# A macaron block on one core: written order for the routing stages' side engines, and an earlier logits' transpose in the attention

## The chip, the core and the metric

The kernel runs on one core of a Trainium2 chip. A core has five engines that run side by side, each with its own list of instructions: TensorE (PE in the profile) for matrix products, VectorE (DVE), ScalarE (ACT), GpSimd (POOL), and SyncE (SP), which here only starts transfers. The engines wait for one another by semaphores. The metric is the time of one execution on the device in microseconds (us), the median of several.

## The reference

The input X has 16 sequences of 256 tokens with 256 channels, in float32: 4096 tokens. The block is a half step of a feed-forward layer, an attention, and another half step of the same feed-forward layer:

```
x = x + 0.5 * ffn(layernorm(x))
x = x + attention(layernorm(x))
x = x + 0.5 * ffn(layernorm(x))
```

The feed-forward layer contains its own input in its output, so that a half step gives x + LN(x)/2 plus half of two sums. It first scales its input h to n = w_norm * h / rms(h). A router takes softmax(n @ w_router) over 32 experts and picks the best four for each token. Each expert takes at most 128 tokens (the first ones in token order; later ones are dropped) and computes silu(n @ w_gate) * (n @ w_up) @ w_down with a width of 176, weighted by the token's probability. A shared expert of width 704 runs over all tokens, weighted by sigmoid(n @ w_shared_gate).

The attention has 16 query heads and 8 key heads of 32 channels, rotary positions on q and k, scores scaled by 1/16 and bent by 50*tanh(s/50), a causal mask, a softmax, and an output projection Wo.

## The kernel before

**Tiles and stages.** The tokens lie in SBUF as 32 tiles x of 128 tokens (NT), in 8 groups of four (NG, GT). The kernel goes through five stages:

1. *First routing stage* (about 0 to 113 us). For each group, `route` (from line 237) computes layernorm statistics on DVE (`moments`, L226 and L227), inverse roots of them on POOL (`root`, L234), and the normed rows xr on DVE (L257). PE transposes xr into pt (L274), and ACT writes that scaled into xnT (L277), from which all matrix products of the layer start. PE makes the router's logits plt (L291); ACT copies them to lt (L296); DVE makes the shared expert's gate by four products with wg (junk, L300). PE transposes the logits to pl (L306), DVE takes the maximum (mx, L308) and subtracts it (ex, L310), ACT takes the exponential (L312), and DVE makes the probabilities and the choice of four (tot L315 to mask L334). `mixed` (L261) makes x + LN(x)/2 in place, by ACT, one instruction for each of the four tiles.
2. *First expert stage* (about 113 to 335 us). With the masks of all groups, PE counts positions (pc, L350), DVE and POOL make the lists of tokens, and each expert's tokens are gathered from a table in memory (xtab) by POOL's indirect DMA, computed (`expert`, pge L467, poe L480) and added back to a sum in memory by another indirect DMA (acc, L483). POOL runs these in written order.
3. *Attention* (about 335 to 800 us). Units (g, b, m) are half of the heads of one sequence. For unit k the loop at line 801 writes: the late sums of unit k−1 (plate, L604), the first part of the scores (sc, L582), the output projection of an earlier unit (poa, L646), projections of the next group (`project`: pq L533, then on DVE a shuffle qs L536, a multiply L540 and further adds), the rest of the scores, and the softmax sums and values of unit k−1 (den and y L628, dT L631, yT L636). Steps of the second layer's routing for groups that are done, `advance(routing.get(...))`, stand between these.
4. *Second expert stage* (from about 809 us), as the first.
5. *Tail*: the sums are read back from memory (a<-acc, L491) and added to x (L495 by POOL, L788 by DVE), and the rest of the shared expert (pg L420, tanh L424, act L425 and L426, po L432, the add into x L436) goes out with the result.

**The shared expert as filler.** The shared expert is a chain of steps without a deadline of their own. The class `Fill` (L657) hands them out in written order: each call of `take(us)` adds to a budget and issues steps until the budget is used up. A step of pg is booked at 3.4, one of po at 2.6. An expert step adds EXPERT_FILL.

**What sets the order.** PE runs in written order throughout (L101). DVE, ACT and POOL run in written order only inside the stack `ordered` (L757 to L882), which covers the attention. POOL also does so in the expert stages. Everywhere else a planner at build time orders DVE's, ACT's and POOL's instructions. Buffers limit this further. PSUM has a ring of two for pg and sc ("big"), one of two named "mm" (pt, po, pq, poa) and one of two named "aux". The logits' tiles plt and pl lie in "aux", but in the second layer's routing, except for its last group, in "mm" (`bank`, L242): the same ring as the projections' pq.

**Lines around the change.** wg, the product of the shared gate's weights with w_norm, is made at line 149 from a copy of w_norm that is loaded into x's last tile. triu, the triangle for the position counts, is made at line 161, and first read by pc. mixed() is called at line 333 in the first layer, and after the first half of the transposes (L283) in the second. Each `yield` in `route` ends one step of it; `feed_forward` (L696) and the attention's loop call the steps.

## Time and profile before

| | us |
|---|---|
| median of three runs | 1091.03 (1089.23 to 1092.94) |
| the profiled execution's own time | 1094.7 |
| its span, first to last instruction | 1093.0 |
| PE busy in it | 1029.6 |
| DVE busy | 647.4 |
| ACT busy | 402.8 |
| POOL busy | 497.1 |
| mean granted clock of PE | 0.981 of full speed |

"L306" in the profile is line 306 of the kernel before. A row like `PE pl L306 <- DVE kT L540` says that PE stood idle ahead of its instruction at line 306 until DVE's at line 540 had ended. A row of the timeline begins with start and length, then names engine, line, operation, and what is written from what; matmuls that follow without a gap are put together (x8), and the bracket is the idle time before the first of them, with what ended it. A window's row gives busy time of each engine in a stretch of time, and PEclk, the share of full clock that PE was granted there.

### The profile page before, as it was taken

How to read it: one execution, taken by the hardware profiler on the slowest of the kernel's cores; microseconds unless marked ns; L12 is line 12 of the kernel's file. 1: busy time of each engine (PE TensorE's matmuls, PEld its weight loads, DVE VectorE, ACT ScalarE, POOL GpSimd, SP SyncE). 2: the span in 40 equal slices, each digit the busy share in tenths (PEclk: the TensorE clock that was granted, in tenths of full speed). 3: DMA queues.
4: the chain of work that ended last, by engine and by line, in shares of the span. 5: the costliest groups of instructions: out<-in, count | busy, mean ns of one | idle time of the engine just before them, and what ended most of it. 6: DMA issues, size and time to landing. Idle time of an engine off the chain costs nothing.

```text
span 1093.0 us, 15757 instructions
## 1 busy us (share of the span) xinstructions
PE 1029.6 (94%) x5448; PEld 633.1 (58%) x5448; DVE 647.4 (59%) x1782; ACT 402.8 (37%) x777; POOL 497.1 (45%) x548
## 2 busy tenths in 40 slices
PE   7799999999999999998989898999899999999988
PEld 4456546776866545444545454555456576867655
DVE  4885664434443546777777868785757644444343
ACT  3343111222220256583738374758221122222101
POOL 3330101555553477786666666574101245555350
PEclk9999999999999999999999999999999999999989
DMA  9631701878862000000101010000300167877380
GB/s 272 201 121 50 238 1 47 174 166 173 176 146 44 19 20 18 3 20 2 41 1 43 1 42 1 23 22 1 97 28 1 33 144 162 179 167 174 49 287 20
DMA packets 137887, 93.13 MB, mean 85 GB/s; under 512 B 80272, under 2 KB 135120, under 8 KB 137808
## 3 DMA queue, kind: packets, MB, share of 16 engines
q1 hardware_dynamic: 125520, 74.29, 24.6%
q0 software_dynamic: 12288, 17.83, 9.5%
q8 instruction: 44, 0.72, 0.3%
q14 instruction: 35, 0.29, 0.1%
HBM read 61.12 MB, written 30.97 MB: 84 GB/s over the span
## 4 chain that ended last, share of the span: by engine, by line
PE 55%; DVE 9%; ACT 2%; DMA 2%; issue 1%; SPq 0%; POOL 0%; DVEq 0%; ACTq 0%; POOLq 0%
PE pg L420 14%; PE po L432 9%; PE pq L533 6%; PE poa L646 5%; PE sc L582 5%; PE pge L467 4%; PE y L628 3%; PE den L628 3%; PE poe L480 2%; DVE st L226 1%; DMA acc<-y,idx 1%; PE pv L561 1%; DVE junk L300 1%; DMA a<-acc 1%; DVE mv L227 1%
## 5 line engine op out<-in xcount | busy, mean ns | idle before, releaser
L420 PE MATMUL pg<-xnT,sw 128*128 128x512 f32 x704 | 320.0, 600 | 4.3 <-DVE act L426 4.3
L420 PEld LDWEIGHTS pg<-xnT,sw 128*128 128x128 f32 x704 | 131.0, 191 | 144.9 <-issue 135.6
L432 PE MATMUL po<-swd,act 128*128 128x256 f32 x768 | 185.3, 393 | 7.9 <-DVE x L436 2.8
L483 POOL DMA_INDIRECT acc<-y,idx x64 | 101.4, 1584 | 178.3 <-DVE y L482 93.6
L432 PEld LDWEIGHTS po<-swd,act 128*128 128x128 f32 x768 | 147.3, 196 | 38.3 <-issue 11.1
L424 ACT ACTIVATE act<-pg 128x512 f32<-128x512 f32 x96 | 57.2, 596 | 299.5 <-PE pg L420 281.5
L425 DVE SCALAR_TENSOR_TENSOR act<-act,pg 128x512 f32<-128x512 f32 x96 | 65.8, 685 | 143.3 <-ACT act L424 117.6
L589 ACT ACTIVATE p<-sc 128x512 f32<-128x512 f32 (+1 forms) x128 | 97.0, 808 | 107.0 <-PE sc L582 106.4
L467 PE MATMUL pge<-xgT,wgu 128*112 128x128 f32 (+1 forms) x768 | 96.1, 275 | 9.3 <-issue 4.8
L594 POOL TENSOR_SCALAR_AFFINE_SELECT p<-p 128x512 f32<-128x512 f32 x128 | 83.7, 677 | 45.1 <-ACT p L592 41.4
L592 ACT ACTIVATE p<-p 128x512 f32<-128x512 f32 (+1 forms) x128 | 100.9, 845 | 0.0
L443 POOL DMA_INDIRECT xg<-xtab,idx x64 | 68.1, 1064 | 71.8 <-DVE idx L397 52.9
L467 PEld LDWEIGHTS pge<-xgT,wgu 128*112 128x112 f32 (+1 forms) x768 | 88.7, 182 | 13.7 <-issue 10.8
L436 DVE SCALAR_TENSOR_TENSOR x<-po,sg,x 128x256 f32<-128x256 f32 x64 | 30.9, 483 | 75.9 <-PE po L432 66.2
L541 POOL TENSOR_TENSOR qs<-qs,kc 128x512 f32<-128x512 f32 x48 | 61.3, 1276 | 20.1 <-DVE qs L536 20.1
L462 ACT ACTIVATE xgT<-pte,wnorm 128x128 f32<-128x128 f32 x128 | 39.7, 365 | 76.6 <-PE pte L459 59.8
L582 PE MATMUL sc<-qT,kT 32*128 32x256 f32 (+1 forms) x512 | 66.3, 550 | 1.7 <-ACT p L589 1.3
L426 DVE TENSOR_TENSOR act<-act,pg 128x512 f32<-128x512 f32 x96 | 65.7, 685 | 2.3
L480 PE MATMUL poe<-wd,sie 112*128 112x256 f32 x256 | 66.0, 380 | 0.9 <-DVE sie L474 0.9
L646 PE MATMUL poa<-wo,yT 128*128 128x256 f32 x256 | 61.6, 394 | 4.4 <-DVE yT L636 3.1
L646 PEld LDWEIGHTS poa<-wo,yT 128*128 128x128 f32 x256 | 48.3, 194 | 22.8 <-DVE yT L636 5.1
L533 PE MATMUL pq<-hT,wq 128*128 128x512 f32 x128 | 60.9, 599 | 0.0
(113 smaller groups left out, 1339.0 us busy)
## 6 DMA issues: line engine op xcount, KB each, us to landing
xtab<-xr SPq DMA_DIRECT2D x16, 576.0 KB
acc<-zero SPq DMA_DIRECT2D x2, 4224.0 KB
a<-acc SPq DMA_DIRECT2D x16, 512.0 KB
wgu<-in_L_ffn_w_gate SPq DMA_DIRECT2D x64, 112.0 KB
wgu<-in_L_ffn_w_up SPq DMA_DIRECT2D x64, 112.0 KB
wd<-in_L_ffn_w_down SPq DMA_DIRECT2D x64, 112.0 KB
wgu<-in_L_ffn_w_gate SPq DMA_DIRECT2D x64, 64.0 KB
wgu<-in_L_ffn_w_up SPq DMA_DIRECT2D x64, 64.0 KB
```

The costliest lines, as they stand in the source:

```text
L420: nc.tensor.matmul(pg[:, s, :], lhsT=sw[:, c, w0 : w0 + P], rhs=xnT[:, c, cols], start=(c == 0), stop=(c == 1))
L432: nc.tensor.matmul(po, lhsT=act[:, k, t * P : (t + 1) * P], rhs=swd[:, k, :], start=(k == 0), stop=(k == len(FC) - 1),)
L443: nc.gpsimd.indirect_dma_start(out=xg, out_offset=None, in_=xtab[n], in_offset=bass.IndirectOffsetOnAxis(ap=idx[:, e : e + 1], axis=0), bo ...
L467: nc.tensor.matmul(pg[:fw, n_, :], lhsT=wgu[:, c, w0 : w0 + fw], rhs=xgT[:, c, :], start=(c == 0), stop=(c == 1))
L480: nc.tensor.matmul(po, lhsT=si[:, k, :], rhs=wd[:, k, :], start=(k == 0), stop=(k == 1))
L483: nc.gpsimd.indirect_dma_start(out=acc[n], out_offset=bass.IndirectOffsetOnAxis(ap=idx[:, e : e + 1], axis=0), in_=y, in_offset=None, boun ...
L533: nc.tensor.matmul(pq, lhsT=weights[:, c, :], rhs=hT[:, c, :], start=(c == 0), stop=(c == 1))
L582: nc.tensor.matmul(sc[i // 2][:, i % 2, 0 : 2 * w].rearrange("p (s t) -> p s t", s=2), lhsT=kT[r, m, t0 + k0 : t0 + k0 + P], rhs=qT[r, m, ...
L589: nc.scalar.activation(parts[h], sc[h][:, :, 0 : 2 * w], AF.Tanh, scale=QK_SCALE / SOFTCAP)
L592: nc.scalar.activation(parts[h], parts[h], AF.Exp, scale=SOFTCAP)
L594: nc.gpsimd.affine_select(out=diag, in_=diag, compare_op=ALU.is_ge, fill=0.0, base=0, pattern=[[0, 4], [1, P]], channel_multiplier=-1,)
L646: nc.tensor.matmul(po, lhsT=yT[:, c // 2, c % 2, qh * P : (qh + 1) * P], rhs=wo[:, c // 2, c % 2, :], start=(c == 0), stop=(c == 3),)
```

## The change

The diff has these edits. EXPERT_FILL goes from 2.15 to 2.3. A tile wn of its own takes w_norm, and the product for wg is written just ahead of the first group's junk. triu is made after the routing loop. In the first layer, mixed() leaves its place between the choice of four and the mask; it becomes a step of its own behind the mask, and is called one group later. In `feed_forward` the whole routing loop runs inside a manual schedule for DVE, ACT and POOL, so that these engines take its instructions in written order. In the attention's loop, the routing step that makes pl, mx and ex stands at j == 2 directly behind the first part of the scores, ahead of the output projection and the projections; at j == 3 the routing step of group g−2 (tot to mask) stays where it was before the last group, and in the last units (k > LAST) it comes ahead of the filler's step.

```diff
-ROUTE_FILL, SLOT_FILL, FIRST_FILL, EXPERT_FILL, SUM_FILL, PROJECT_FILL = 2.0, 1.7, 6.0, 2.15, 17.0, 1.5
+ROUTE_FILL, SLOT_FILL, FIRST_FILL, EXPERT_FILL, SUM_FILL, PROJECT_FILL = 2.0, 1.7, 6.0, 2.3, 17.0, 1.5
...
-    nc.sync.dma_start(x[:, NT - 1, :], w_norm.unsqueeze(0).to_broadcast([P, C]))
-    nc.vector.tensor_mul(wg, wg, x[:, NT - 1, :])
+    rows0 = ExitStack()
+    xrows = rows0.enter_context(tc.tile_pool(name="rows0", bufs=3, side="right"))
+    wn = xrows.tile([P, C], F32, name="wn", bufs=1)
+    nc.sync.dma_start(wn, w_norm.unsqueeze(0).to_broadcast([P, C]))
...
-    nc.vector.tensor_single_scalar(triu, const("iota"), slot, ALU.is_ge)
...
         nc.scalar.copy(lt, plt)
+        if n == 0 and g == 0:
+            nc.vector.tensor_mul(wg, wg, wn)
         for t in range(GT):
...
-        if n == 0:
-            mixed()
         nc.vector.tensor_single_scalar(
             mask[:, :, g * GT : (g + 1) * GT], hit[:, :, 0:E].rearrange("p t e -> p e t"), 1.5, ALU.is_gt
         )
         yield 0.0
+        if n == 0:
+            mixed()
+            yield 0.0
...
-        for g, work in works.items():
...
-            advance(work, 1 + n)
-            advance(later[1])
...
+        with tc.manual_schedule(engines={ET.DVE, ET.Activation, ET.Pool}):
+            for g, work in works.items():
...
+                advance(work, 1 + n)
+                advance(works.get(g - 1))
+                advance(later[1])
...
+            advance(work, 1 - n)
         if n == 0:
             routed.close()
+
+            nc.vector.tensor_single_scalar(triu, const("iota"), slot, ALU.is_ge)
             clear(0)
             load_attention()
...
                 next(parts)
+            if j == 2:
+                advance(routing.get(g - 2))
             if k >= 2 and units[k - 2][2] == 1:
                 d = units[k - 2][:2]
                 project_out(*d, outs.pop(d))
             advance(mine, PROJECT_PIECES[j][0])
             if k == LAST:
                 fill2.step()
-            if j == 2:
-                advance(routing.get(g - 2))
...
+            if j == 3 and k > LAST:
+                advance(routing.get(g - 2))
...
-            if j == 3:
+            if j == 3 and k < LAST:
                 advance(routing.get(g - 2))
```

More of the change, by code (lines that the diff above doesn't have):

```diff
@@ L696, in feed_forward @@
     def feed_forward(n, pool, works, fill, routed=None):
-        for g, work in works.items():
-            later = [works.get(g + d) for d in range(3)]
-            next(work)
-            if g == 0:
-                next(later[1])
-            fill.take(ROUTE_FILL)
-            advance(work, 1 + n)
-            advance(later[1])
-            if n == 0 and g == 0:
-                warm(WARM[1])
-            fill.take(ROUTE_FILL)
-            next(work)
-            fill.ready = g + 1
-            fill.take(LOGIT_FILL)
-            advance(work, 2)
-            advance(later[2])
-            fill.take(ROUTE_FILL)
-            next(work)
+        with tc.manual_schedule(engines={ET.DVE, ET.Activation, ET.Pool}):
+            for g, work in works.items():
+                later = [works.get(g + d) for d in range(3)]
+                next(work)
+                if g == 0:
+                    next(later[1])
+                fill.take(ROUTE_FILL)
+                advance(work, 1 + n)
+                advance(works.get(g - 1))
+                advance(later[1])
+                if n == 0 and g == 0:
+                    warm(WARM[1])
+                fill.take(ROUTE_FILL)
+                next(work)
+                fill.ready = g + 1
+                fill.take(LOGIT_FILL)
+                advance(work, 2)
+                advance(later[2])
+                fill.take(ROUTE_FILL)
+                next(work)
+            advance(work, 1 - n)
         if n == 0:
             routed.close()
+            nc.vector.tensor_single_scalar(triu, const("iota"), slot, ALU.is_ge)
             clear(0)
@@ L749, in macaron_kernel @@
     with tc.tile_pool(name="ffn0", bufs=1) as pool:
-        rows0 = ExitStack()
-        xrows = rows0.enter_context(tc.tile_pool(name="rows0", bufs=3, side="right"))
         first = {g: route(0, g, xrows) for g in range(NG)}
```

## The prediction

> **What bounds the kernel now.** I read the busy shares first, then what ended TensorE's idle time, then the lines around the longest of those waits, and last the granted clock in short windows.

> ```profile
> PE 1029.6 (94%) x5448; PEld 633.1 (58%) x5448; DVE 647.4 (59%) x1782; ACT 402.8 (37%) x777; POOL 497.1 (45%) x548
> ```

> TensorE (PE) is busy for 1029.6 of 1093.0 us; no other engine passes 60%. The diff takes no matmul away, so it can act only on PE's 63 us of idle time and on the stretches at half clock. The waits of PE (total, times, longest) name the idle places:

> ```profile
> PE pl L306 <- DVE kT L540: 14.5, 5, 3.3
> ...
> PE pg L420 <- DVE act L426: 4.3, 2, 3.5
> ...
> PE poa L646 <- DVE yT L636: 3.1, 1, 3.1
> PE po L432 <- DVE x L436: 2.8, 1, 2.8
> ...
> PE po L432 <- ACT xnT L277: 2.1, 1, 2.1
> PE pc L350 <- DVE mask L334: 1.6, 1, 1.6
> ```

> The diff touches each of them: the first in the attention, the third where the attention ends, the po behind x in the tail, the rest in the first routing stage.

> **1. Attention: pl (the logits' transpose) goes ahead of the projections.** Of the five places I show the one at 561, PE and then VectorE (DVE); columns are start, length, engine, line.

> ```profile
> 561.00 0.33 PE L306 MATMUL pl<-kc,lt 128*128 128x128 f32 x1 [3.32 <-DVE kT L540]
> 561.26 1.24 PE L582 MATMUL sc<-qT,kT 32*128 32x256 f32 x8
> 559.66 0.72 DVE L536 STREAM_SHUFFLE qs<-pq 128x512 f32<-128x512 f32 x1
> 560.27 0.67 DVE L540 TENSOR_TENSOR kT<-pq,kc 128x512 f32<-128x512 f32 x1
> 562.40 0.29 DVE L310 TENSOR_TENSOR ex<-pl,mx 128x128 f32<-128x128 f32 x1
> ```

> pl and the projections' tiles pq share a PSUM ring of two. Today the order on the ring is pq of k, pq of the first q, pl; pl must wait until kT's multiply (L540) has read the first of them. That multiply stands on DVE behind eight pairs of layernorm statistics and the late sums' add (plate, L604), whose end at 559.66 I call P. The scores' second part stands behind pl on PE and starts at P + 1.60.

> After the change the order is pl, pq of k, pq of q. pl finds a free bank and its own 3.32 us go. But now the q projection takes pl's bank, so it waits until pl's readers mx (L308) and ex (L310) are done. DVE keeps its written order: v's copy, the eight statistics pairs, plate, and only then mx and ex. They end at P + 0.28 + 0.04 + 0.29 = P + 0.61. The q projection then starts at about P + 0.66; its group of four takes 1.82 (the k group's start at 553.98 to the q group's at 555.80); the scores come behind it on PE, at P + 2.48 instead of P + 1.60. So the stall does not go: it moves from pl to q, and what follows starts 0.88 later. Queued behind it on PE are the second scores, den and y, and behind those DVE's dT, which already sits 3.28 us waiting for den; nothing later takes the 0.88 back. Four places have a stall of 3.32, one of 1.22. Five times 0.88 is **+4.4**. A gain of the 14.5 us would need mx and ex ahead of the statistics on DVE, which the written order excludes. The bound above is a q group that, now first behind the gap, runs at half rate on top of today's loss: 1.82 in four places, +7.

> Clock. After these stalls the windows show the granted clock halved (window, length, busy of PE, PEld, DVE, ACT, POOL, then PEclk):

> ```profile
> 562.00:563.00 1.00, 1.00 (x16) 0.34 (x12) 0.65 (x3) 0.41 (x1) 0.97 (x3) 0.50 0.00 0
> 1056.00:1059.00 3.00, 3.00 (x9) 2.37 (x8) 0.42 (x1) 0.00 (x0) 0.00 (x0) 0.50 1.09 385
> ```

> The first follows an idle of 3.32, the second an idle of 2.85; after the one of 1.22 at 714 the clock stayed at 1.00. [...] By the rows they have paid this already, since sc, den and y near 561 run 1.3 to 1.7 us longer than at undisturbed places; only the fifth, at 1.22 + 0.88 = 2.10, is new. The measurement decides: I take **+0.4** for that one (a quarter of 1.5), and keep 0 and +1.5.

> **2. First routing stage (0 to 113 us).** Two of its PE stalls, the second that which ends the stage:

> ```profile
> 24.56 5.40 PE L420 MATMUL pg<-xnT,sw 128*128 128x512 f32 x8 [3.54 <-DVE act L426]
> 113.20 0.30 PE L350 MATMUL pc<-triu,mask 128*32 128x128 bf16 x8 [1.60 <-DVE mask L334]
> ```

> Listing all over 0.8 us (3.54, 1.78, 0.87, 1.57, 2.12, 1.60, small ones) gives about 13 us, and about 4.4 us more at half clock. DVE decides most of them. A window from 17.75 to 113.20 has DVE busy 71.65 of 95.45, idle 23.8. Today the planner mixes independent instructions of different groups; in written order an instruction follows the one that it depends on, as it already does in the attention, so I take the elapsed times of the written rows there: statistics 0.53 a tile, four gate products (junk) 1.83, four xr 1.38, act pair 1.34, mx and ex 0.61, tot to mask 2.80, an add of po 0.46. From xr of group 1 to the mask of group 7 the DVE has 7 × 1.38 + 8 × 1.83 + 8 × 0.61 + 24 × 0.53 + 8 × 2.80 + 14 × 1.34 + 9 × 0.46 + about 1.3 for the rest = 88.5, so 17.75 + 88.5 = 106.2 with no idle. It must still wait for the first tanh, for xnT and for PE; I put 8 us on that (an estimate: a third of today's 23.8, whose shares for act and po alone are 7.1 and 8.3). The last mask then ends near 114.2, where pc starts at 113.20 today: **+1.0**. On PE the stalls would sit elsewhere: 3.4 at the second pg (its tanh is served after xr), about 4 near 42 and 3.6 near 86, where the first po tile needs act of its last chunk behind junk, ex and a group's statistics. Ends: −3 if DVE's idle shrinks to 4, +3 if it is 10. The scaled x + LN(x)/2 (ScalarE, about 2.08 a group) only leaves the way of tanh and xnT by a group; ScalarE is busy 37.49 of 95.45, so it costs nothing unless po waits for x, and x is due only at the group's po, later still. The product for wg moves 0.4 us of DVE, its own tile frees x's last tile; triu moves 0.28 behind the loop. The queue of SP gets the same loads in the same order.

> **3. EXPERT_FILL 2.15 to 2.3.** It brings 34 × 0.15 = 5.1 units of shared work forward in each FFN. Two or three expert steps that had no filler get one; such steps show PE waits of 0.4 to 1.0. In the first FFN: **−1.0** (ends 0 and −2). One po tile (2.6 us) is then missing as filler near 405, where PE waits 1.1 for ScalarE: kept for the range, +0.5.

> **4. End of the attention and last routing group.**

> ```profile
> 769.32 0.69 DVE L425 SCALAR_TENSOR_TENSOR act<-act,pg 128x512 f32<-128x512 f32 x1 [2.15 <-ACT act L424]
> 775.97 4.54 PE L646 MATMUL poa<-wo,yT 128*128 128x256 f32 x12 [3.15 <-DVE yT L636]
> 790.81 2.08 ACT L265 ACTIVATE x<-x,xb,xa 128x256 f32<-128x256 f32 x4 [1.23 <-DVE xr L257]
> ```

> Behind the last units, tot to mask now runs ahead of the filler's step, in DVE's 2.15 of idle at 769. It no longer stands between act and dT, so yT ends 2.0 earlier and poa's wait falls from 3.15 to about 1.1; poa's twelve then run at full clock, 2.62 instead of 4.54. Together −3.9. Afterwards ScalarE's written order puts the four instructions of line 265 (2.08) behind a tanh and ahead of xnT; today the planner has them earlier. plt then waits about 2.6 where PE waited 0.74 and 0.27: +1.6. If that gap halves the clock, up to +1.7 more; [...]by the row of 2.85 it can. −2.3 or −0.6: I take **−1.5**.

> **5. Tail.**

> ```profile
> 1033.11 1.56 POOL L483 DMA_INDIRECT acc<-y,idx  x1 [2.86 <-DVE act L426]
> 1051.08 2.02 DVE L788 TENSOR_TENSOR x<-x,a 128x256 f32<-128x256 f32 x1 [5.04 <-DMA a<-acc]
> 1053.55 5.49 PE L432 MATMUL po<-swd,act 128*128 128x256 f32 x12 [2.85 <-DVE x L436]
> ```

> PE's last expert matmuls start at 1026.15, but the 32 scatters, 4.89 us apart on average, run 5 to 6 us behind; the last at 1033.11 sets when the sums come back (1051.0) and the last po start (1053.55). More filler per step delays the experts' own matmuls: 4.4 us at the end of PE's part, of which POOL's lag takes 3.5 to 3.9. **+0.7** (ends 0 and +3). What the second FFN's steps gain is lost in this chain.

> **Sum.** 4.4 + 0.4 + 1.0 − 1.0 − 1.5 + 0.7 = +4.0. The profiled execution took 1094.7 (its span of 1093.0 and 1.7 around it), so 1098.7 for its like; it lies 3.7 above the median of 1091.03, so the median becomes 1095.0.

> **Rivals.**
> - *Faster: written order really takes the stalls out of the routing stage.* Place: 0 to 113 us. For it: 13 + 4.4 us are there to be had, and ScalarE's due work goes ahead of x + LN(x)/2. Against it: the 88.5 us of DVE work. Price: DVE idle of 1 instead of 8 us puts the mask at 107, −6, and part 4 at −3.9 without a new plt wait is 2.4 better than mine; 4.0 − 7 − 2.4 = −5.4, so 1085.6. It decides (a fall of 3.3) once the mask ends by 109.3, with DVE idle for no more than 3.1 us.
> - *No change that can be told: the moved stall is no longer than the old.* It needs the q group to start while plate still runs, by 0.9 us, or scores that don't stand behind it; the written order speaks against both. Part 1 is then 0.4 alone and the sum −0.4: 1090.6.
> - *Slower still: new stalls lose the clock.* The gaps near 23, 42 and 86, of 3.4 to 4, and plt's are each followed by half clock: 4 × 1.5 = +6 against the 4.4 lost at half clock in the routing stage today, of which only a part comes back: +4 to +6 more, 1099 to 1101.

> **How the numbers follow.** About 0.3% (3.3 us) can be told from no change. Likeliest case (0.52): 1095.0, own range 1092 to 1098; about 0.30 of the whole is its part above 1094.3. Faster: 0.17. No change by a stall that keeps its length: 0.08. Slower still: 0.23. So faster 0.17, within 0.22 + 0.08 = 0.30, slower 0.30 + 0.23 = 0.53. The range reaches to the far side of two rivals, 1087 to 1101.5; about 0.1 lies beyond each end.

> **What would show it.** Right: PE's wait for kT at pl is gone and five waits of a pq for DVE's ex stand in its place, 15 to 19 us in total; second scores start 2.5 after plate; pc starts near 114; poa's wait is near 1.1 and plt waits over 2 for xnT; the tail's po still starts behind the sums' return. Wrong: pc before 110; no wait at pq; or new half-clock windows after 23, 42 and 86 with pc beyond 117. What would upset all of it is a planner that orders the other queues differently around the routing stage than the row counts here suggest.

## The result and the profile after

| | us |
|---|---|
| median of six runs, changed | 1099.46 (1097.14 to 1101.73) |
| median of six runs, before | 1091.42 (1089.23 to 1093.16) |
| changed / before | 1.0071, 95% interval 1.0053 to 1.0089 |
| profiled execution of the changed kernel | 1098.06, span 1096.4 |

The change makes the kernel slower by 0.71%, or 7.8 us (0.0071 × 1091.42; 5.8 to 9.7 by the interval). The forecast was +4.0.

The line of busy times and the waits of TensorE (total, times, longest) in the changed kernel:

```profile
PE 1032.0 (94%) x5448; PEld 632.5 (58%) x5448; DVE 655.8 (60%) x1782; ACT 402.8 (37%) x777; POOL 494.0 (45%) x548
```

```profile
PE pq L536 <- DVE ex L312: 17.8, 5, 4.0
PE po L435 <- DVE act L429: 6.3, 4, 3.3
...
PE pg L423 <- DVE act L429: 2.9, 2, 2.7
PE plt L291 <- ACT xnT L277: 2.5, 2, 2.2
PE pc L353 <- DVE mask L334: 2.4, 1, 2.4
...
PE po L435 <- DVE x L439: 1.3, 1, 1.3
...
PE poa L649 <- DVE yT L639: 1.1, 1, 1.1
```

The line of 14.5 us at pl is gone, and one of 17.8 us at pq stands in its place, again five times. The wait of poa for yT fell from 3.1 to 1.1. In the routing stage the waits have changed places and not shrunk: up to pc, PE is idle for 16.0 us, against 14.7 before.

The timeline of the changed kernel at the first of the five places, PE and then DVE:

```profile
502.83 0.33 PE L308 MATMUL pl<-kc,lt 128*128 128x128 f32 x1
503.28 1.98 PE L536 MATMUL pq<-hT,wk 128*128 128x512 f32 x4
509.26 3.75 PE L536 MATMUL pq<-hT,wq 128*128 128x512 f32 x4 [3.99 <-DVE ex L312]
512.94 1.24 PE L585 MATMUL sc<-qT,kT 32*128 32x256 f32 x8
507.39 1.19 DVE L607 TENSOR_TENSOR plate<-p,p 128x1024 f32<-128x1024 f32 x1
508.82 0.29 DVE L312 TENSOR_TENSOR ex<-pl,mx 128x128 f32<-128x128 f32 x1
```

pl no longer waits. The q projection waits 3.99 us until ex has read pl's bank, and its four matmuls then take 3.75 us where four took 1.88 before: they run at half clock. Two windows show it, at the first and the second of the five places (the value behind ACT's and POOL's busy times, 0.50, is the granted clock):

```profile
508.46:515.28 6.82, 6.02 (x24) 2.29 (x28) 3.13 (x9) 1.01 (x3) 6.33 (x12) 0.50 0.00 1
566.48:569.89 3.41, 3.41 (x12) 0.98 (x10) 1.29 (x4) 0.00 (x0) 3.24 (x6) 0.50 0.02 5
```

From the start of the instruction behind the first scores to the den behind plate, the five places take longer by 2.41 (13.59 for 11.18), 1.04, 2.40, 1.02 and 1.02 us: 7.9 in this trace. About 1.02 of each is the longer way over ex. The other 1.4 at the first and the third place come with a half clock of 6.82 us there, where it lasts 3.41 at the second and the fourth, and at each of the four before.

The first routing stage, PE, and DVE ahead of PE's start at 89.58:

```profile
24.49 6.72 PE L423 MATMUL pg<-xnT,sw 128*128 128x512 f32 x8 [2.66 <-DVE act L429]
89.58 1.19 PE L435 MATMUL po<-swd,act 128*128 128x256 f32 x2 [3.34 <-DVE act L429]
117.62 0.29 PE L353 MATMUL pc<-triu,mask 128*32 128x128 bf16 x8 [2.38 <-DVE mask L334]
87.54 0.40 DVE L226 BATCH_NORM_STATS2 st<-x 128x6 f32<-128x256 f32 x1
88.75 0.69 DVE L429 TENSOR_TENSOR act<-act,pg 64x512 f32<-64x512 f32 x1
```

The last act stands behind a group's statistics on DVE, and PE's po waits for it. pc starts at 117.62, 4.4 us later than at 113.20 before. A window over this stage shows DVE busy (the third pair) for 87.05 us, against 78.84 before, and a mean clock of 0.91 against 0.95. The changed kernel, then the kernel before:

```profile
0.00:117.60 117.60, 101.62 (x432) 59.50 (x432) 87.05 (x372) 42.46 (x101) 28.84 (x75) 0.91 0.50 151
0.00:113.20 113.20, 98.53 (x432) 56.95 (x432) 78.84 (x373) 42.77 (x101) 31.51 (x75) 0.95 0.52 158
```

The end of the attention, the last routing group and the tail:

```profile
784.88 2.86 PE L649 MATMUL poa<-wo,yT 128*128 128x256 f32 x12 [1.15 <-DVE yT L639]
806.74 0.77 PE L291 MATMUL plt<-xnT,wr 128*32 128x128 f32 x12 [2.23 <-ACT xnT L277]
807.45 1.98 PE L423 MATMUL pg<-xnT,sw 128*128 128x512 f32 x4
1059.90 2.86 PE L435 MATMUL po<-swd,act 128*128 128x256 f32 x12 [1.32 <-DVE x L439]
```

poa runs at full clock now (its twelve in 2.86 us, 4.54 before), and plt waits 2.23 us for xnT. In the tail the last po waits less than in the trace before (1.32 for 2.85) and keeps its clock (its twelve in 2.86 us for 5.49); a second trace of the kernel before, below, shows that this is in part chance.

One trace is one execution, and executions of one kernel differ: from the first pc to the first poa, two traces of the kernel before took 311.9 and 314.1 us. So times below are given as ratios over all runs of both kernels, with a 95% interval, and traces are read only within a stage. Where a microsecond stands for a ratio, it is the ratio's distance from 1 times the median before.

### The profile page after: what moved, and what is told of

Read it like the earlier page. It is cut to its first block, busy times and chain, and to the rows that moved or that the text cites. A ratio compares the mean times of both kernels' runs of the same rounds, so it can differ in the third digit from the quotient of the medians.

```text
span 1096.4 us, 15768 instructions
## 1 busy us (share of the span) xinstructions
PE 1032.0 (94%) x5448; PEld 632.5 (58%) x5448; DVE 655.8 (60%) x1782; ACT 402.8 (37%) x777; POOL 494.0 (45%) x548
## 4 chain that ended last, share of the span: by engine, by line
PE 79%; DVE 12%; ACT 3%; issue 2%; DMA 2%; SPq 1%; POOL 1%; ACTq 0%; DVEq 0%; POOLq 0%
PE pg L423 24%; PE po L435 15%; PE pge L470 8%; PE pq L536 7%; PE poa L649 5%; PE poe L483 5%; PE sc L585 5%; PE y L631 3%; PE den L631 3%; DVE st L226 2%; DVE act L428 1%; DVE junk L302 1%; PE pte L462 1%; DVE act L429 1%; DVE mv L227 1%
## 5 line engine op out<-in xcount | busy, mean ns | idle before, releaser
L536 PE MATMUL pq<-hT,wq 128*128 128x512 f32 x128 | 67.3, 653 | 17.8 <-DVE ex L312 17.8
L483 PE MATMUL poe<-wd,sie 112*128 112x256 f32 x256 | 66.0, 380 | 1.6 <-DVE sie L477 0.9
L233 POOL TENSOR_SCALAR s<-mv 128x4 f32<-128x4 f32 x40 | 9.5, 237 | 125.4 <-DVE mv L227 123.8
```

Of the source, the lines that this page charges most:

```text
L483: nc.tensor.matmul(po, lhsT=si[:, k, :], rhs=wd[:, k, :], start=(k == 0), stop=(k == 1))
L536: nc.tensor.matmul(pq, lhsT=weights[:, c, :], rhs=hT[:, c, :], start=(c == 0), stop=(c == 1))
```

## The experiments

**The earlier pl alone.** The kernel before with this edit:

```diff
                 next(parts)
+            if j == 2:
+                advance(routing.get(g - 2))
             if k >= 2 and units[k - 2][2] == 1:
...
-            if j == 2:
-                advance(routing.get(g - 2))
             if mine is None and j % 2 == 0:
```

> The kernel before with one edit: pl, mx and ex directly behind the first scores. Theory of the forecast (the stall moves from pl to the first q projection and its group runs in the half clock that follows): five waits of pq for ex of 4.0, 4.0, 4.0, 4.0 and 1.9 us, and by the trace of the whole change +2.4, +1.0, +2.4, +1.0, +1.0 at the five places, in all +5 to +8 us. Rival (the attention has slack behind it, and the longer time of the whole change comes from the routing stage alone): within 2 us of before.

Measured: 1098.23 against 1092.91, ratio 1.0046 (1.0028 to 1.0064): +5.0 us (3.1 to 7.0). Its trace has the same five waits of pq for ex, 17.8 us in total. So this one edit makes most of the loss, and the rival falls. From the first place's start to the fifth's end, the three traces with pl early and the statistics in their old place take 223.8 to 225.2 us, and seven with both in their old places 215.8 to 217.6: 7.7 more in the mean. At the end of the kernel the interval allows no more than 7.0; where the rest is taken back is not shown.

**Where the stall comes from.** In the kernel before, DVE does eight statistics between v's copy and plate, at the place at 561 from 554.30 to 558.54, and later waits for den:

```profile
554.30 0.41 DVE L226 BATCH_NORM_STATS2 st<-x 128x6 f32<-128x256 f32 x1
558.54 1.19 DVE L604 TENSOR_TENSOR plate<-p,p 128x1024 f32<-128x1024 f32 x1
565.97 0.72 DVE L631 STREAM_TRANSPOSE dT<-den 128x512 f32<-128x512 f32 x1 [3.28 <-PE den L628]
```

If the stall is these 4.24 us, it must go when they move, wherever pl stands. The statistics of the routing (`route`'s first step) and of the next projection go behind the second scores of unit j == 2:

```diff
                 probs[u] = next(parts)
+            if j == 2 and g >= 1:
+                routing[g - 1] = route(1, g - 1, rows)
+                next(routing[g - 1])
+                fill2.ready = max(g - 1, 0)
+            if j == 2:
+                advance(ahead)
...
-            if j == 1 and g >= 1:
+            if j == 1 and g == NG:
                 routing[g - 1] = route(1, g - 1, rows)
...
-            elif j < 2:
+            elif j == 0:
                 advance(ahead)
```

> The kernel before, with the eight layernorm statistics of an attention group (four of the routing, four of the next projection) taken from the end of unit j == 1 to unit j == 2, behind the second scores, where DVE waits 3.3 us for den; pl stays where it was before. Theory (the stall at pl is the statistics' 4.25 us ahead of plate and kT's multiply): PE's wait at pl falls from 14.5 us to under 2, the half clock behind it goes too, -12 to -20 us. Rival (the wait moves to den and yT, since the statistics then stand ahead of dT): pl's wait is gone and the time within 4 us of before.

> The same move of the statistics, with pl directly behind the first scores as in the change. Theory (what the edit of pl costs is only that mx and ex stand behind the statistics and plate): the wait of pq for ex falls from 17.8 us to under 4 and the time is within 3 us of the run with pl in its old place. Rival (pl's early place costs by itself, by the ring of two): slower than that run by 4 us or more.

Measured with pl in its old place: 1079.35 against 1093.17, ratio 0.9870 (0.9845 to 0.9896), −14.2 us. With pl early: 1078.92, ratio 0.9873 (0.9833 to 0.9913). Neither trace has a wait of PE for kT at pl or for ex at pq. The timeline with pl in its old place, PE and then DVE:

```profile
556.69 1.88 PE L533 MATMUL pq<-hT,wq 128*128 128x512 f32 x4
558.40 0.27 PE L306 MATMUL pl<-kc,lt 128*128 128x128 f32 x1
558.61 0.71 PE L582 MATMUL sc<-qT,kT 32*128 32x256 f32 x8
564.07 0.40 DVE L226 BATCH_NORM_STATS2 st<-x 128x6 f32<-128x256 f32 x1
564.60 0.68 DVE L631 STREAM_TRANSPOSE dT<-den 128x512 f32<-128x512 f32 x1
```

q, pl and the scores follow one another at full clock (the scores take 0.71 us, 1.24 before). The statistics now end where dT begins; DVE stood idle for 3.28 us there before. Once the statistics are moved, the place of pl is worth nothing that can be told: both ratios agree.

**The routing stage in written order.** Only the first layer's loop is changed, with the later x + LN(x)/2 and the moves of wg and triu:

```diff
+        with ExitStack() as written:
+            if n == 0:
+                written.enter_context(tc.manual_schedule(engines={ET.DVE, ET.Activation, ET.Pool}))
...
+                advance(works.get(g - 1))
...
-        if n == 0:
-            mixed()
...
         yield 0.0
+        if n == 0:
+            mixed()
+            yield 0.0
```

> The kernel before with the first routing stage in written order on DVE, ACT and POOL, x + LN(x)/2 a group later, wg and triu moved; nothing else. Theory of the forecast, with the trace of the whole change: DVE is the bound, pc starts at 117.6 instead of 113.2, and all of it passes to the end, +3.5 to +5 us. The forecast's own sum was +1.0. Rival (the expert stage absorbs a late start of pc, since its transfers are ahead): pc late by 4.4 but the end by less than 1.5 us.

Measured: 1094.53 against 1092.91, ratio 1.0013 (0.9998 to 1.0028): +1.4 us (−0.2 to +3.1). In its trace pc starts at 118.8 and DVE is busy for 87.10 us up to there, as in the changed kernel. By the medians the end is late by less than pc is in the trace. But the traced execution took 1098.4 us, 3.9 more than this kernel's median, so its pc need not be the usual one.

**Which engine's order does it.** The same kernel with ACT and POOL in written order and DVE left to the planner, and the same kernel with no engine in written order:

```diff
-                written.enter_context(tc.manual_schedule(engines={ET.DVE, ET.Activation, ET.Pool}))
+                written.enter_context(tc.manual_schedule(engines={ET.Activation, ET.Pool}))
```

> As the run with the routing stage in written order, but DVE is left to the planner; only ACT and POOL are in written order. Theory (DVE's written order is what makes the stage longer, by dependent instructions in a row): DVE busy up to pc is under 81 us instead of 87, pc starts at 112 to 115, the time within 1.5 us of before. Rival (ACT's order or the later x + LN(x)/2 does it): pc at 117 or later.

> The kernel before with x + LN(x)/2 behind the mask and a group later, wg and triu moved, and no engine in written order in the routing stage. Theory (the gain of the run with ACT and POOL in written order comes from that order, which puts tanh and xnT ahead of x + LN(x)/2): pc at 111 to 114 and the time within 3 us of before. Rival (the later place of x + LN(x)/2 does it alone, whatever orders ACT): pc near 106, -7 to -10 us.

Measured with ACT and POOL in written order: 1084.18 against 1093.17, ratio 0.9917 (0.9896 to 0.9937), −9.1 us. With none: 1091.87 against 1093.37, ratio 0.9977 (0.9963 to 0.9991), −2.5 us, with pc at 114.3. The first of the two, its PE, its first tanh and the first x + LN(x)/2 behind it on ACT, and its window up to pc:

```profile
22.29 5.40 PE L423 MATMUL pg<-xnT,sw 128*128 128x512 f32 x8 [1.82 <-DVE act L429]
14.78 0.60 ACT L427 ACTIVATE act<-pg 128x512 f32<-128x512 f32 x1 [3.33 <-PE pg L423]
23.80 2.08 ACT L265 ACTIVATE x<-x,xb,xa 128x256 f32<-128x256 f32 x4
```

```profile
0.00:106.10 106.10, 97.72 (x432) 56.69 (x432) 78.72 (x373) 42.55 (x101) 30.00 (x75) 0.97 0.56 169
```

And the kernel before, ACT up to the same first tanh:

```profile
21.42 1.09 ACT L265 ACTIVATE x<-x,xb,xa 128x256 f32<-128x256 f32 x2 [3.84 <-DVE st L226]
22.42 0.57 ACT L424 ACTIVATE act<-pg 128x512 f32<-128x512 f32 x1
```

The planner had put two instructions of x + LN(x)/2 (line 265) ahead of the tanh that PE waits for. They wait for DVE's statistics until 21.42, so that ACT stands idle for 3.84 us, although the tanh's pg had ended by 15.8. In written order the tanh runs at 14.78, as soon as its pg is done. With no engine in written order the planner places the two ahead of the tanh again (22.29 and 23.29), so the later place alone does not free it. PE's wait falls from 3.54 to 1.82 us, and pc comes at 106.1, 7.1 us earlier than before. ACT's and POOL's orders were not tried apart. What the 2.5 us of the run with none come from is not shown.

DVE is busy for 78.7 us with the planner and 87.1 in written order, for the same work. The instructions are not longer: the lengths of all that start ahead of pc add up to 103.1 us in the kernel before and 103.5 in the changed one. What differs is how neighbours overlap. Two rows of the changed kernel, then three of the kernel before:

```profile
61.65 0.39 DVE L226 BATCH_NORM_STATS2 st<-x 128x6 f32<-128x256 f32 x1
62.07 0.18 DVE L227 BATCH_NORM_AGGREGATE mv<-st 128x2 f32<-128x6 f32 x1
65.58 0.42 DVE L226 BATCH_NORM_STATS2 st<-x 128x6 f32<-128x256 f32 x1
65.92 0.28 DVE L320 TENSOR_TENSOR ex<-ex,tot 128x128 f32<-128x128 f32 x1
66.11 0.18 DVE L227 BATCH_NORM_AGGREGATE mv<-st 128x2 f32<-128x6 f32 x1
```

In written order mv needs the st just ahead of it and starts 0.03 us after that has ended. The planner puts an independent instruction between, which starts 0.08 before st's end, and mv then starts 0.09 before that one's. These 8.4 us are the larger part of what DVE's written order puts on pc: 12.7 us from this run to the run before it (106.1 to 118.8), and 11.3 in the changed kernel, as the repaired versions below show (106.3 to 117.6). So the change holds a gain in the order of ACT and POOL and loses it again by DVE's.

**The other two parts alone.** EXPERT_FILL at 2.3, and the step of j == 3 with the last routing group in written order:

```diff
-ROUTE_FILL, SLOT_FILL, FIRST_FILL, EXPERT_FILL, SUM_FILL, PROJECT_FILL = 2.0, 1.7, 6.0, 2.15, 17.0, 1.5
+ROUTE_FILL, SLOT_FILL, FIRST_FILL, EXPERT_FILL, SUM_FILL, PROJECT_FILL = 2.0, 1.7, 6.0, 2.3, 17.0, 1.5
```

> The kernel before with EXPERT_FILL at 2.3 and nothing else. Theory of the forecast: -1.0 from the first expert stage and +0.7 from the tail, in all -0.3 us, within 1.5 us of before. Rival (the tail's last po no longer falls behind an idle gap that halves the clock, as in the trace of the whole change): -3 to -5 us.

```diff
+            if j == 3 and k > LAST:
+                advance(routing.get(g - 2))
...
-            if j == 3:
+            if j == 3 and k < LAST:
                 advance(routing.get(g - 2))
...
+        with ExitStack() as written:
+            if n:
+                written.enter_context(tc.manual_schedule(engines={ET.DVE, ET.Activation, ET.Pool}))
```

> The kernel before with the routing step of j == 3 ahead of the filler's step in the last units, and the last routing group in written order; nothing else. Theory of the forecast: poa's wait for yT falls from 3.1 to 1.1 and loses its half clock (-3.9), plt waits over 2 us for xnT (+1.6 or more), in all -1.5 to -2.5 us. Rival (the tail is set by the scatters and not by what is ahead, so that nothing of it reaches the end): within 0.5 us of before.

Measured: 1093.20 for the fill, ratio 0.9998 (0.9984 to 1.0013), and 1093.16 for the end, ratio 1.0003 (0.9987 to 1.0019), both against 1092.91. Neither moves the time by more than about 2 us. The tail of the kernel with the fuller steps:

```profile
1052.76 5.39 PE L432 MATMUL po<-swd,act 128*128 128x256 f32 x12 [4.36 <-DVE x L436]
```

PE has less shared work left behind the experts, comes to the last po earlier, and waits there for the sums. This wait is 4.0 to 5.8 us in three of the four traces with EXPERT_FILL at 2.3 (1.3 in that of the change), and 1.5 to 2.9 in the ten with 2.15. In the other run poa's wait fell to 1.15 as foreseen and the last poa started at 776.4 instead of 780.1; but the last pc started at 815.9 instead of 816.5. Between them plt waited, and the clock was halved behind it:

```profile
796.09 0.84 PE L291 MATMUL plt<-xnT,wr 128*32 128x128 f32 x12 [2.23 <-ACT xnT L277]
796.85 3.57 PE L420 MATMUL pg<-xnT,sw 128*128 128x512 f32 x4
```

**A second trace of the kernel before.** The same kernel with one constant added that nothing uses, so that no instruction changes.

> The kernel before once more, for a second trace of it. Theory (the end of the run varies from one execution to the next): the wait of the last po for x and the half clock behind it differ from the first trace's 2.85 and 5.49 us by over 1 us, with the attention the same within 0.5 us. Rival: the tail is the same within 0.5 us, and the spread lies in the loads at the start.

Measured: 1092.18, one run. The wait at pl is 14.5 us again, and the tail another:

```profile
1054.02 2.86 PE L433 MATMUL po<-swd,act 128*128 128x256 f32 x12 [1.56 <-DVE x L437]
```

1.56 and 2.86 instead of 2.85 and 5.49: 3.9 us less. So part of the first trace's tail was chance.

**Repaired versions.** The changed kernel with DVE left to the planner in the routing loop; then that kernel with the statistics moved as well; then the kernel before with only these two edits.

> The changed kernel with DVE taken out of the manual schedule of the routing loop, all else as in the change. Theory (DVE's written order in the first routing stage turns a gain of 9 us into a loss of 1.4; the rest of the change costs what it cost before): pc near 106 and the time 1088 to 1091, 2 to 5 us faster than before. Rival (the gains in front are swallowed by the tail as soon as other parts are late): within 1.5 us of before, or slower.

> The changed kernel with DVE left to the planner in the routing loop and the statistics of the attention moved behind the second scores. Theory (both gains add): -14 and -9 us, in all 1068 to 1073. Rival (the scatters of the second expert stage and the read back of the sums set the end by then): pc of the second layer 20 us earlier but the end by less than 17 us.

> The kernel before with the same two edits only: ACT and POOL in written order in the first routing stage (with x + LN(x)/2 a group later), and the statistics of the attention moved; EXPERT_FILL 2.15, pl in its old place. Theory (the change's other parts are worth nothing once these two are in): within 3 us of the changed kernel with the same edits. Rival (the earlier pl or the fuller expert steps pay once the stall is gone): 4 us or more behind it.

Measured, against 1093.37: 1092.48, ratio 0.9992 (0.9979 to 1.0005); 1072.39, ratio 0.9798 (0.9772 to 0.9825); 1072.06, ratio 0.9817 (0.9791 to 0.9842). The first is not told apart from before, where 2 to 5 us less were expected: against the ratio 1.0071 of the change it gains about 0.8%, with its pc at 106.3, and in its tail the last po waits 4.04 us. Whether the tail swallows part of the gain in front, as the rival has it, stays open: such waits go with the fuller expert steps. The other two beat the kernel before by 22.1 us (19.1 to 24.9) and 20.0 (17.3 to 22.8), close to the 14.2 + 9.1 of the two gains alone, so these add. In the trace of the second, the last pc comes 24.2 us earlier than before and the end 22.6, against its rival. Their intervals overlap: EXPERT_FILL, the early pl and the moved step are worth nothing that these runs can tell. In the second the last po waits long again, in the third for 1.6 us, at the same median; the second's:

```profile
1032.07 4.74 PE L435 MATMUL po<-swd,act 128*128 128x256 f32 x12 [5.81 <-DVE x L439]
```

## Why the prediction was right, and where it was off

Direction and range held: +7.8 us, where +4.0 was forecast and the range went to 1101.5. The size was about half. The likeliest case was 1092 to 1098, and the measured 1099.5 lies where the rival "Slower still" was put, 1099 to 1101. Step by step:

- **Step 1, pl.** Right in mechanism. The stall moved to the q projection, behind ex, as worked out from the ring of two and DVE's order: 3.99 us where 4.20 was foreseen, and 1.88 at the fifth place where it was 2.10. Moving the statistics away showed that they are its cause. The term was 4.4 + 0.4. At the end of the kernel, this part alone gave +5.0 (3.1 to 7.0), which does not refute it; at the five places it was more, 7.9 in the trace of the change and 7.7 in the mean of all traces. Of the 7.9, five times 1.02 answer to the 4.4. The rest, 2.8, is the clock, for which I took 0.4: I held that the half clock was paid already and added it for the fifth place alone. That place kept its clock (its q group took 1.95 us); what came instead is a second stretch of 3.41 us at half clock at two of the first four. The upper bound, a q group at half rate on top of today's loss in all four, is not what happened: behind the other two q groups (3.16 and 3.09 us) the half clock ended within the scores, while in the trace before it lasted through den and into y.
- **Step 2, routing stage.** Right that DVE, in written order, takes up its own idle time and more, and that the stage gains nothing. Mis-sized: pc at 117.6, not 114.2. I let DVE start xr of group 1 at 17.75; it starts at 19.51 (19.14 in the trace before). And idle time, with my 88.5 us of work, comes to 117.6 − 19.5 − 88.5 = 9.6, not 8. In time, the part alone is +1.4 (−0.2 to +3.1), where the term was +1.0. Why a pc that is 4.4 to 5.6 us late in two traces costs so little at the median stays open; one of the two is of an execution 3.9 above its median, and seven traces of kernels with the old routing stage spread over 2.1 us at pc (112.1 to 114.2).
- **Step 3 with step 5, the fill.** −1.0 + 0.7 = −0.3 was forecast, −0.2 (−1.7 to +1.4) measured. That gains of the second expert stage are lost to the scatters is supported by the longer wait of po (4.36, and 4.0 and 5.8 in two other traces with the fuller steps).
- **Step 4, end of the attention.** Right in mechanism, too favourable in size: −1.5 was forecast, +0.3 (−1.4 to +2.1) measured. Its first half came true (poa 3.7 us earlier in that part's trace, for 3.9). I had taken the middle of two branches, −2.3 with full clock behind plt's wait and −0.6 with half. Both exist: from the fifth place to the last pc, the run of this part alone is 0.5 us shorter than before, with four pg in 3.57 instead of 1.98 us behind a wait of 2.23, and the changed kernel 2.5 shorter, with full clock behind the same wait.
- **The sum.** The four parts alone add to 5.0 + 1.4 − 0.2 + 0.3 = 6.5 us, the whole to 7.8 (5.8 to 9.7); the rest is within the intervals. The anchor was sound at the median. The first trace of the kernel before, on which I worked, had 3.9 us more at the last po than the second. Stage by stage, the trace of the change differs from it by +4.4 up to the first pc (forecast +1.0), −1.4 from there to the first of the five places (−1.0), +7.9 to the end of the fifth (+4.8), −2.5 to the last pc (−1.5) and −5.1 behind it (+0.7). These add to +3.4, near the +4.0, by luck: the tail that was long by chance hides what the terms of the routing stage and of the five places lack.
- **The rivals.** The faster one, "written order really takes the stalls out", came half true, and is the larger lesson: with ACT and POOL in written order and DVE not, pc was at 106.1, where its price had been worked out with 107. I had treated the three engines as one edit. "The moved stall is no longer than the old" is refuted by the five waits. "Slower still" came closest. Its sign, new half clock after 23, 42 and 86 with pc beyond 117, is in the trace of the change: half clock from 20.4 to 30.6, from 47.7 to 51.1 and from 88.6 to 95.4, in all twice the 10.2 us of the trace before, and pc at 117.6. It missed the attention, where the same happens at two places; and at the median the routing stage costs 1.4 us alone, so that most of the loss is the attention's.

## What to carry to other kernels

When a wait sits on a shared ring of buffers, moving the waiting instruction ahead can hand the wait to the next user of its slot, as here; look for what stands in front of the slot's reader on its engine, and move that into a later idle gap of the same engine (here −14 us for eight statistics at each place). Decide between planner and written order for each engine by itself: ScalarE and GpSimd together gained, by serving the tanh that TensorE waits for first, while VectorE lost, since the planner put independent instructions, which here started 0.08 us ahead of their neighbour's end, between dependent ones, which started 0.03 us behind it (78.7 against 87.1 us busy). And ahead of a tail that waits for a chain of transfers, the extra filler here brought nothing (−0.2 us) and moved the idle time.

## What the runs showed of the hardware

The length of a wait alone did not decide the clock here. The same wait of plt, 2.23 us, was followed by four pg in 1.98 us in the changed kernel and in 3.57 us in the run of the end alone, and q groups behind equal waits of 3.99 us took from 3.09 to 3.75 in the changed kernel.

```profile
793.25:796.66 3.41, 1.18 (x19) 0.47 (x17) 2.78 (x9) 3.14 (x7) 0.00 (x0) 1.00 0.00 0
796.66:800.08 3.42, 3.42 (x8) 1.41 (x5) 0.23 (x2) 0.27 (x1) 0.00 (x0) 0.50 0.00 0
802.00:805.41 3.41, 2.52 (x13) 1.08 (x11) 0.97 (x2) 1.63 (x4) 0.00 (x0) 1.00 0.00 0
805.41:808.82 3.41, 2.08 (x15) 0.98 (x16) 2.04 (x9) 1.91 (x5) 0.00 (x0) 1.00 0.00 0
808.82:812.24 3.42, 3.42 (x16) 2.54 (x15) 1.95 (x4) 0.66 (x2) 0.00 (x0) 1.00 0.00 0
```

In the first kernel the whole wait falls into one step, with PE idle for 2.23 of 3.41 us, and the next step runs at half clock. In the second the edge at 805.41 cuts it: 0.89 and 1.33 us idle, and the clock stays. Counted over the two traces: all 15 steps at full clock with 1.8 us idle or more were followed by half clock, as were 4 of the 15 with 1.31 to 1.78, and none with 1.26 or less. Of 26 steps at half clock, the 7 with 0.65 us idle or more were followed by another, and the 19 with 0.53 or less were not. These are counts of two executions; they do not show where a limit lies. The four waits of 3.3 us at pl in the trace before lost one step each; of the four of 3.99 us at pq in the changed kernel, two lost one and two lost two; and the waits at the fifth place, 1.22 and 1.88 us, kept the clock.
